# Second-layer blocks, a table load and a score bound moved inside the window-attention layer of a four-layer convolution kernel

## The chip, the cores and the metric

The kernel runs on one core of a Trainium2 chip. The metric is the device time of one execution in microseconds (us), lower being better. The engines are called by the profile's names: PE (TensorE matmuls) and PEld (its weight loads), DVE (VectorE), ACT (ScalarE), POOL (GpSimd) and SP (SyncE, which issues transfers).

## The reference, cut to what matters

Four layers run one after the other on x, of 4 images, 16 channels, 512 x 512, in fp32. Only layer 0 is touched by the change:

```python
pos = depthwise_conv3x3(x)                   # per channel
x = x + pos + pos_b
win = windows_of_8x8(affine(x))              # 64 tokens each
q, k, v = qkv(win)                           # 2 heads of 8 channels
out = softmax(q @ k.T) @ v                   # scores, exp, sums, division
x = x + proj(out)
h1 = gelu(affine(x) @ fc1_w.T + fc1_b)       # first layer, 16 -> 64
x = x + h1 @ fc2_w.T + fc2_b                 # second layer, 64 -> 16
```

Layer 1 rounds its input to 8 bits, which needs the maximum of |x| over the whole output of layer 0, then a 3x3 convolution with batch statistics. Layer 2 is two 3x3 convolutions with a residual, layer 3 a 3x3 convolution and a two-layer network with a residual.

## The kernel before

Layer 0 is `window_attention`. It takes the exponentials of the scores without subtracting a maximum first; a bound on the scores, computed on the chip from the weights and from the largest |y| seen, says at the end whether that was safe. `values_load` reads this `flag` on the engines, and a branch (L147) would run the slower `attention_block` if it weren't. Then `conv_layers` does layers 1 to 3.

The work of layer 0 is cut into 64 steps. A step n holds, for all 4 images (`u`) and 8 strips of rows (4 pairs, `vv`), one row of 8 windows. PSUM has 8 banks: banks 0 to 3 are two pairs of two, banks 4 to 7 single ones. PE, DVE, ACT and SP run the program in the order in which the Python code issues it (`manual_schedule`). A step is issued in this order:

- **Head of the step.** A table load for exp and ln (`preload_act_table_set`, L470), `values(0)` (four transposes, L346, into bank 4, copied by DVE, L351), and `scores(0)` (16 matmuls, L359, over banks 0 to 3, then two ACT exps of a pair each, L367).
- **The rest of the step before.** `output(*last)`: the second layer of image 3 of step n - 1.
- **Attention.** For k = 1 to 7: `scores(k)`, `attend(k - 1)` (L378, and the sums, L383), `values(k)`, `divide(k - 1)` (L392 to L394). In between, `turn_keys` (L318) writes the next step's keys by DMA into `y2`, and `queries` (L328) makes its queries. `project` (L402, L407) adds the result to y.
- **Second part.** 52 items go to PE in a row: 36 are depthwise taps of step n + 2 (L295, into banks 0 to 3), 16 are groups of the first layer (`hidden`, L416, each 4 matmuls into banks 4, 5, 6 in turn, and an ACT gelu, L421). Item i uses partition group i mod 4. After first-layer groups 5 and 9 stands an `output` of one image: four matmuls of 128 rows (L427) into bank 7, a DVE add to y (L429).
- **Seam.** `position(n + 2)` takes the depthwise sums out of banks 0 to 3, images 0 and 2 on DVE (L310), 1 and 3 on ACT (L306). Then comes the `output` of image 2, and the next step begins.

After the add in an odd step, `store` takes a maximum (L438) and `_store_block` issues some 16 to 19 transfers of 32 KB to `x1` from SP (L96) per image; the last step's stores are 76. Each matmul in fp32 shows as two records, so the profile counts eight L427 records per image.

Of the kernel before, what the change touches and what calls it, by code (L numbers as in the profile page):

```python
# [1 line left out]

# [9 lines left out]
F32 = mybir.dt.float32  # L12
BF16 = mybir.dt.bfloat16
AF = mybir.ActivationFunctionType
ALU = mybir.AluOpType
AX = mybir.AxisListType
# [8 lines left out]
P = 128  # L25
# [5 lines left out]
NH, HD = 2, 8  # L31
WS = 8
# [51 lines left out]
        nc.sync.dma_start(part[:, at : at + m, :], src[:, a : a + m, :])  # L84


def _store_block(nc, x1, src, b, r0, cols):

    n = WS // 2
    s, m = divmod(r0 // 2, M)  # L90
    parts = [(1, m, s, 0, n), (0, m + 1, s, 0, n)]
    if m + n == M and s < S - 1:
        parts[1:] = [(0, m + 1, s, 0, n - 1), (0, 0, s + 1, n - 1, 1)]
    for r, mm, ss, at, k in parts:
        part = 32 * b + C * r
        nc.sync.dma_start(  # L96
            x1[mm : mm + k, part : part + C, ss, cols].rearrange("m c x -> c m x"),
            src.rearrange("c (m r) x -> c m r x", r=2)[:, at : at + k, 1 - r],
        )
# [53 lines left out]
def window_attention(ctx: ExitStack, tc, xw, x1, hots, m, v, peak):  # L153
# [14 lines left out]
    nc = tc.nc  # L168
    U = V = 4
    BW = 64  # L170
    NJ = BW // WS
    N = NJ * T
    XW = 2 * BW
    SR = H // 8
    NQ = W // XW
    STEPS = SR // WS * NQ * 2

    wts = ctx.enter_context(tc.tile_pool(name="w0w", bufs=1))
# [5 lines left out]
    def bank(i):  # L184
        return pairs[i // 2][:, i % 2, :] if i < 4 else singles[i - 4]

    def quad(i):
        return slice(32 * i, 32 * i + 32)
# [43 lines left out]
    with tc.tile_pool(name="w0s", bufs=1) as scratch:  # L232
# [10 lines left out]
        size = wts.tile([P, NH + 1], F32, name="size")  # L243
# [27 lines left out]
    px = ctx.enter_context(tc.tile_pool(name="w0x", bufs=2))  # L271
# [10 lines left out]
    most = pa.tile([P, STEPS], F32, name="most")  # L282

    def by_window(ap):
        return ap.rearrange("p (j a x) -> p a j x", a=WS, x=WS)
# [29 lines left out]
    def turn_keys(y, vv):  # L315
        for u in range(U):
            for w in range(2):
                nc.sync.dma_start(  # L318
                    y2[32 * u + C * w : 32 * u + C * w + C, vv, :, w, :],
                    y[32 * vv + C * w : 32 * vv + C * w + C, u, :].rearrange(  # L320
                        "p (j t) -> p j t", t=T
                    ),
                )

    def queries(y, h):
        for u in range(U):
            for vv in range(V):
                nc.tensor.matmul(  # L328
                    bank(vv)[quad(u)], wg[h][quad(vv)], y[quad(vv), u, :],
                    start=True, stop=True,  # L330
                )
        for vv in range(V):
            out = g[:, vv, :, h, :]
            src = bank(vv).rearrange("p (j t) -> p j t", t=T)
            if vv % 2:
                nc.scalar.activation(out, src, AF.Identity, bias=gb[:, h : h + 1])
            else:
                nc.vector.tensor_scalar(out, src, gb[:, h : h + 1], None, ALU.add)


    def values(k, n):

        vv, jl = k // 2, 4 * (k % 2)
        b = bank(4 + 2 * (k % 2))
        for jj in range(4):
            nc.tensor.transpose(  # L346
                b[:, P * jj : P * jj + P],
                y2[:, vv, jl + jj].rearrange("p w t -> p (w t)"), m("ident"),
            )
        t = px.tile([P, 4, P], F32, tag="yt", name=f"yt{n}_{k}", bufs=3)  # L350
        nc.vector.tensor_copy(t.rearrange("p j c -> p (j c)"), b)  # L351
        return t
# [45 lines left out]
    def project(y):  # L398
        for h in range(NH):
            for u in range(U):  # L400
                for vv in range(V):
                    nc.tensor.matmul(  # L402
                        bank(4 + u)[quad(vv)], wo[h][quad(u)], o[quad(u), vv, :, h, :],
                        start=h == 0, stop=h == 1,
                    )
        for u in range(U):
            nc.vector.scalar_tensor_tensor(  # L407
                y[:, u], bank(4 + u), pb, y[:, u], ALU.add, ALU.add
            )

    def hidden(y, q, n):

        u, vv = q // 4, 3 * q % 4
        b = bank(4 + q % 3)
        for k in range(4):
            nc.tensor.matmul(  # L416
                b[quad(k)], fc1[quad(vv), quad(k)], y[quad(vv), u, :],
                start=True, stop=True,
            )
        hd = px.tile([P, N], F32, tag="hid", name=f"hid{n}_{u}_{vv}", bufs=8)  # L420
        nc.scalar.activation(hd, b, AF.Gelu, bias=f1b)  # L421
        return vv, hd

    def output(y, xo, hids, u, n):
        b = bank(7)
        for vv, hd in hids:
            nc.tensor.matmul(b[quad(vv)], m("fc2"), hd, start=True, stop=True)  # L427
        at = BW * (n % 2)
        nc.vector.tensor_tensor(  # L429
            xo[:, u, :, at : at + BW].rearrange("p a (j x) -> p a j x", x=WS),  # L430
            by_window(b), by_window(y[:, u]), ALU.add,
        )
        if n % 2:
            store(xo, n // 2, u)

    def store(xo, k, u):
        i, cb = divmod(k, NQ)
        nc.vector.tensor_reduce(  # L438
            peak[:, U * k + u : U * k + u + 1], xo[:, u], AX.XY, ALU.max,
            apply_absolute_value=True,  # L440
        )
        for vv in range(V):
            for w in range(2):
                r = SR * (2 * vv + w) + WS * i
                _store_block(
                    nc, x1, xo[32 * vv + C * w : 32 * vv + C * w + C, u], u, r,
                    slice(XW * cb, XW * cb + XW),
                )

    ctx.enter_context(  # L450
# [14 lines left out]
    for h in range(NH):  # L465
        queries(ys[0], h)
    last, xo = None, None
    for n in range(STEPS + 1):
        if n < STEPS:
            nc.scalar.preload_act_table_set("natural_log_exp_and_others")  # L470
            yts = {0: values(0, n)}
            es = {0: scores(0, n)}
        if last:

            output(*last)
        if n == STEPS:
            break
        for k in range(1, 8):
            es[k] = scores(k, n)
            attend(es[k - 1], yts[k - 1], k - 1)  # L480
            yts[k] = values(k, n)
            divide(k - 1, n)
            if k == 3:
                nc.vector.tensor_reduce(
                    most[:, n : n + 1], ys[n], AX.XY, ALU.max, apply_absolute_value=True
                )
            if k % 2 and n + 1 < STEPS:
                turn_keys(ys[n + 1], k // 2)
        if n + 1 < STEPS:
            queries(ys[n + 1], 0)  # L490
        attend(es[7], yts[7], 7)
        divide(7, n)
        if n + 1 < STEPS:
            queries(ys[n + 1], 1)
        y = ys.pop(n)
        project(y)

        ahead = n + 2 < STEPS
        if ahead and n % 2 == 0 and n // 2 + 2 < STEPS // 2:
            xts[n // 2 + 2] = load(n // 2 + 2)  # L500
        if n % 2 == 0:
            xo = px.tile([P, U, WS, XW], F32, tag="xo", name=f"xo{n}", bufs=1)


        hids, taken = [], [0] * U
        for i in range(13 * 4):
            q, rest = divmod(i - 4, 3)
            if i >= 4 and rest == 0 and q < 16:
                hids.append(hidden(y, q, n))
                if q in (5, 9):  # L510
                    output(y, xo, hids[q - 5 : q - 1], q // 4 - 1, n)
            elif ahead:
                depthwise(n + 2, taken[i % 4], i % 4)
                taken[i % 4] += 1
        if ahead:
            ys[n + 2] = position(n + 2)
        output(y, xo, hids[8:12], 2, n)
        last = (y, xo, hids[12:], U - 1, n)

    top = wts.tile([P, 1], F32, name="top")
    nc.vector.tensor_reduce(top, most, AX.X, ALU.max)
    ytop = wts.tile([P, 1], F32, name="ytop")
    nc.gpsimd.partition_all_reduce(ytop, top, P, bass_isa.ReduceOp.max)
    sized = wts.tile([P, NH + 1], F32, name="sized")
    nc.gpsimd.partition_all_reduce(sized, size, P, bass_isa.ReduceOp.add)
    bound = wts.tile([P, 1], F32, name="bound")
    nc.vector.tensor_tensor(bound, sized[:, 0:1], sized[:, 1:2], ALU.max)
    nc.vector.tensor_scalar(bound, bound, ytop, sized[:, 2:3], ALU.mult, ALU.add)  # L530
    nc.vector.tensor_scalar(bound, bound, ytop, 1.0 / 8.0, ALU.mult, ALU.mult)
    flag = wts.tile([P, 1], mybir.dt.int32, name="flag")
    nc.vector.tensor_scalar(flag, bound, 40.0, None, ALU.is_le)
    return nc.values_load(flag[0:1, 0:1], min_val=0, max_val=1)


# [798 lines left out]
```

## Time and profile before

| What | Value |
|---|---|
| Median of 3 runs | 6498.27 us (6492.53 to 6499.6) |
| The profiled execution's own time | 6499.56 us |
| Its span, first to last instruction | 6497.8 us |
| Mean granted PE clock | 0.981 |
| PE busy | 6264.0 us (96%) |
| ACT busy | 4179.7 us (64%) |
| DVE busy | 3186.5 us (49%) |
| POOL busy | 6.0 us |
| A step of layer 0 | 54.16 us (1612.33 to 1666.49) |
| Layer 0 | until about 3538 us, then layers 1 to 3 from 3561 us |

The span has 40 slices of 162 us; layer 0 fills the first 21 and a half. A timeline row gives the start of a group of like instructions, the time from its first start to its last end, the engine, the line, the operation, the tile written and read, the count and, in brackets, how long the engine sat idle before it and who released it. The busy share of PE counts a matmul from start to a modelled end, so a PE that is nearly always busy may still be used in part[...].

### The profile page before, as it was taken

How to read it: one execution, taken by the hardware profiler on the slowest of the kernel's cores; microseconds unless marked ns; L12 is line 12 of the kernel's file. 1: busy time of each engine (PE TensorE's matmuls, PEld its weight loads, DVE VectorE, ACT ScalarE, POOL GpSimd, SP SyncE). 2: the span in 40 equal slices, each digit the busy share in tenths (PEclk: the TensorE clock that was granted, in tenths of full speed). 3: DMA queues.
4: the chain of work that ended last, by engine and by line, in shares of the span. 5: the costliest groups of instructions: out<-in, count | busy, mean ns of one | idle time of the engine just before them, and what ended most of it. 6: DMA issues, size and time to landing. Idle time of an engine off the chain costs nothing. (4 is left out here: it accounts for less than half of the span.)

```text
span 6497.8 us, 317055 instructions
## 1 busy us (share of the span) xinstructions
PE 6264.0 (96%) x146976; PEld 3402.1 (52%) x146976; DVE 3186.5 (49%) x4640; ACT 4179.7 (64%) x5738; POOL 6.0 (0%) x26
## 2 busy tenths in 40 slices
PE   8999999999999999999997669999999999999999
PEld 5555555555555555555553335455555554555553
DVE  3444444444444444444443974544445554545554
ACT  5777777777777777777775544555555555555554
POOL 0000000000000000000000000000000000000000
PEclk9999999999999999999997879999999999999999
DMA  3333333333333333333322842222222222222221
GB/s 82 62 71 62 71 63 70 63 70 63 70 63 70 63 70 62 71 61 72 60 56 61 298 161 75 81 82 86 83 82 81 82 83 82 84 83 81 81 65 48
DMA packets 544390, 515.30 MB, mean 79 GB/s; under 512 B 349008, under 2 KB 480208, under 8 KB 514384
## 3 DMA queue, kind: packets, MB, share of 16 engines
q1 hardware_dynamic: 542768, 494.52, 29.2%
q8 instruction: 1154, 18.91, 1.2%
q14 instruction: 180, 1.47, 0.1%
q10 hardware_dynamic: 288, 0.39, 0.0%
HBM read 225.87 MB, written 134.48 MB: 55 GB/s over the span
## 5 line engine op out<-in xcount | busy, mean ns | idle before, releaser
L1123 ACT ACTIVATE hid<-tb,vec 128x512 f32<-128x512 f32 x1280 | 847.5, 687 | 1127.8 <-PE tb L1117 1126.5
L1117 PE MATMUL tb<-y,mat 32*32 32x512 f32 x16384 | 1567.9, 599 | 2.0 <-DVE o L1139 1.3
L367 ACT ACTIVATE e<-pair 128x1024 f32<-128x1024 f32 x1024 | 992.3, 1021 | 225.0 <-PE pair L359 224.3
L1125 DVE TENSOR_SCALAR hid<-tb,vec 128x512 f32<-128x512 f32 x768 | 575.3, 749 | 890.0 <-PE tb L1117 872.8
L295 PE MATMUL pair<-x,taps 32*32 32x512 f32 x18432 | 965.8, 605 | 1.9 <-ACT y L306 1.3
L416 PE MATMUL bank<-y,fc_e 32*32 32x512 f32 x8192 | 878.4, 607 | 3.7 <-ACT hid L421 3.2
L421 ACT ACTIVATE hid<-bank,f1b 128x512 f32<-128x512 f32 x1024 | 679.6, 686 | 298.8 <-PE bank L416 285.3
L351 DVE COPY yt<-bank 128x512 f32<-128x512 f32 x512 | 353.8, 691 | 906.1 <-PE bank L346 905.8
L359 PE MATMUL pair<-g,y 32*128 32x128 f32 x16384 | 651.2, 285 | 40.4 <-ACT e L367 39.3
L1117 PEld LDWEIGHTS tb<-y,mat 32*32 32x32 f32 x16384 | 496.4, 103 | 329.4 <-issue 185.0
L908 PE MATMUL tb<-z,cw 32*32 32x512 f32 x12864 | 640.4, 603 | 4.2 <-ACT z L1054 3.4
L359 PEld LDWEIGHTS pair<-g,y 32*128 32x128 f32 x16384 | 540.2, 186 | 186.8 <-ACT e L367 109.2
L908 PE MATMUL tb<-x,cw 32*32 32x512 f32 x12480 | 620.0, 597 | 1.5 <-ACT z L1054 1.5
L295 PEld LDWEIGHTS pair<-x,taps 32*32 32x32 f32 x18432 | 459.3, 103 | 286.3 <-issue 182.9
L908 PE MATMUL tb<-h,cw 32*32 32x512 f32 x12672 | 590.7, 601 | 1.8 <-ACT z L1054 1.5
L378 PE MATMUL bank<-e,yt 128*32 128x128 f32 x16384 | 555.3, 276 | 0.9 <-ACT r L393 0.9
L908 PE MATMUL tb<-q,cq 32*32 32x512 bf16 x12672 | 418.5, 424 | 138.4 <-ACT q L987 103.2
L383 PE MATMUL bank<-e,hot 128*32 128x512 f32 x4096 | 535.0, 593 | 0.0
L378 PEld LDWEIGHTS bank<-e,yt 128*32 128x32 f32 x16384 | 417.6, 109 | 108.1 <-DVE yt L351 52.8
L1133 PE MATMUL tb<-hid,mat 128*32 128x512 f32 x4096 | 471.1, 601 | 0.0
L429 DVE TENSOR_TENSOR xo<-bank,y 128x512 f32<-128x512 f32 x256 | 177.1, 692 | 547.2 <-PE bank L427 545.5
L346 PEld LDWEIGHTS bank<-mat,y 128*128 128x128 f32 x2048 | 215.3, 141 | 431.7 <-issue 378.1
(150 smaller groups left out, 6661.2 us busy)
## 6 DMA issues: line engine op xcount, KB each, us to landing
tx<-x SPq DMA_DIRECT2D x128, 1024.0 KB
x<-in_xw_dram SPq DMA_DIRECT2D x32, 2600.0 KB
y<-y SPq DMA_DIRECT2D x2048, 32.0 KB
xi<-x SPq DMA_DIRECT2D x1024, 64.0 KB
out_dram<-o SPq DMA_DIRECT2D x64, 1024.0 KB
x<-xo SPq DMA_DIRECT2D x2000, 32.0 KB
tx<-x SPq DMA_DIRECT2D x4, 768.0 KB
x<-xo SPq DMA_DIRECT2D x48, 24.0 KB
```

What stands on the lines that cost most here:

```text
L295: nc.tensor.matmul(bank(u)[quad(vv)], taps[quad(u), tap, :], xts[n // 2][quad(u), vv, dy : dy + WS, at : at + BW], start=tap == 0, stop=ta ...
L359: nc.tensor.matmul(bank(u)[:, P * jj : P * jj + P], y2[quad(u), vv, jl + jj].rearrange("p w t -> p (w t)"), g[quad(u), vv, jl + jj].rearra ...
L367: nc.scalar.activation(e[:, 2 * i : 2 * i + 2].rearrange("p u j t -> p u (j t)"), pairs[i], AF.Exp,)
L378: nc.tensor.matmul(b[quad(u), P * jj : P * jj + P], yt[:, jj, quad(u)], e[:, u, jj, :], start=True, stop=True,)
L383: nc.tensor.matmul(d[quad(u)], own, e[:, u].rearrange("p j t -> p (j t)"), start=True, stop=True,)
L416: nc.tensor.matmul(b[quad(k)], fc1[quad(vv), quad(k)], y[quad(vv), u, :], start=True, stop=True,)
L421: nc.scalar.activation(hd, b, AF.Gelu, bias=f1b)
L908: nc.tensor.matmul(p[i][_quad(j)], weights[_quad(i), side, dx, :], src[side][_quad(i), j, dx : dx + W], start=side == 0 and dx == 0, stop= ...
L1117: nc.tensor.matmul(p[_quad(c)], w1[_quad(b), 1 - par, 32 * c : 32 * c + 32], inner(ys(mm + par))[_quad(b), s, :], start=True, stop=True,)
L1123: nc.scalar.activation(hd, p, AF.Relu, bias=v("l3_b1"))
L1125: nc.vector.tensor_scalar(hd, p, v("l3_b1"), 0.0, ALU.add, ALU.max)
L1133: nc.tensor.matmul(p[_quad(b), :], w2[:, par], hd, start=par == 0, stop=par == 1)
```

## The change

It has five parts, all in layer 0.

- `output` takes several images and banks at once. In the second part the outputs of images 1 and 0 stand together after first-layer group 10, into banks 6 and 7, in place of one after group 5 and one after group 9. `hid` gets 12 buffers instead of 8.
- Image 2's output leaves the end of the step and stands with image 3's behind the next step's `scores(0)`, into banks 6 and 7.
- The table load for exp and ln is issued behind the last gelu, ahead of `position(n + 2)`, instead of at the head of the next step.
- The score bound (`bounded`) is computed behind `project` of the last step instead of after all steps.
- The stores of the last step alternate between the queues of SP and POOL.

```diff
-def _store_block(nc, x1, src, b, r0, cols):
+def _store_block(nc, x1, src, b, r0, cols, queues=None):
...
-        nc.sync.dma_start(
+        (next(queues) if queues else nc.sync).dma_start(
...
-        hd = px.tile([P, N], F32, tag="hid", name=f"hid{n}_{u}_{vv}", bufs=8)
+        hd = px.tile([P, N], F32, tag="hid", name=f"hid{n}_{u}_{vv}", bufs=12)
...
-    def output(y, xo, hids, u, n):
-        b = bank(7)
-        for vv, hd in hids:
-            nc.tensor.matmul(b[quad(vv)], m("fc2"), hd, start=True, stop=True)
+    def output(y, xo, hids, us, banks, n):
+
+        for k, (vv, hd) in enumerate(hids):
+            nc.tensor.matmul(
+                bank(banks[k // 4])[quad(vv)], m("fc2"), hd, start=True, stop=True
+            )
         at = BW * (n % 2)
-        nc.vector.tensor_tensor(
-            xo[:, u, :, at : at + BW].rearrange("p a (j x) -> p a j x", x=WS),
-            by_window(b), by_window(y[:, u]), ALU.add,
-        )
-        if n % 2:
-            store(xo, n // 2, u)
+        for u, i in zip(us, banks):
+            nc.vector.tensor_tensor(
+                xo[:, u, :, at : at + BW].rearrange("p a (j x) -> p a j x", x=WS),
+                by_window(bank(i)), by_window(y[:, u]), ALU.add,
+            )
+            if n % 2:
+                store(xo, n // 2, u)
+
+    def bounded():
...
+        nc.vector.tensor_reduce(top, most, AX.X, ALU.max)
+        ytop = wts.tile([P, 1], F32, name="ytop")
+        nc.gpsimd.partition_all_reduce(ytop, top, P, bass_isa.ReduceOp.max)
...
+        return flag
+
+
+    queues = itertools.cycle((nc.sync, nc.gpsimd))
...
-                    slice(XW * cb, XW * cb + XW),
+                    slice(XW * cb, XW * cb + XW), queues if k == STEPS // 2 - 1 else None,
...
     last, xo = None, None
+    nc.scalar.preload_act_table_set("natural_log_exp_and_others")
     for n in range(STEPS + 1):
         if n < STEPS:
-            nc.scalar.preload_act_table_set("natural_log_exp_and_others")
             yts = {0: values(0, n)}
             es = {0: scores(0, n)}
...
         project(y)
+        if n + 1 == STEPS:
+            flag = bounded()
...
-                if q in (5, 9):
-                    output(y, xo, hids[q - 5 : q - 1], q // 4 - 1, n)
+                if q == 10:
+
+
+                    output(y, xo, hids[4:8] + hids[0:4], (1, 0), (4 + 8 % 3, 7), n)
...
+        if n + 1 < STEPS:
+            nc.scalar.preload_act_table_set("natural_log_exp_and_others")
         if ahead:
             ys[n + 2] = position(n + 2)
-        output(y, xo, hids[8:12], 2, n)
-        last = (y, xo, hids[12:], U - 1, n)
...
+        last = (y, xo, hids[8:], (2, 3), (6, 7), n)
+
     return nc.values_load(flag[0:1, 0:1], min_val=0, max_val=1)
```

The removed block after the loop is the body that `bounded` now holds, with the same operations. The added import of `itertools` moves every later line by one; some lines move by more.

More of the change, by code (lines that the diff above doesn't have):

```diff
@@ L1 @@
+import itertools
 from contextlib import ExitStack
@@ L419, in hidden @@
             )
-        hd = px.tile([P, N], F32, tag="hid", name=f"hid{n}_{u}_{vv}", bufs=8)
+        hd = px.tile([P, N], F32, tag="hid", name=f"hid{n}_{u}_{vv}", bufs=12)
         nc.scalar.activation(hd, b, AF.Gelu, bias=f1b)
         return vv, hd
-    def output(y, xo, hids, u, n):
-        b = bank(7)
-        for vv, hd in hids:
-            nc.tensor.matmul(b[quad(vv)], m("fc2"), hd, start=True, stop=True)
-        at = BW * (n % 2)
-        nc.vector.tensor_tensor(
-            xo[:, u, :, at : at + BW].rearrange("p a (j x) -> p a j x", x=WS),
-            by_window(b), by_window(y[:, u]), ALU.add,
-        )
-        if n % 2:
-            store(xo, n // 2, u)
+    def output(y, xo, hids, us, banks, n):
[3 more added lines that the diff above has]
+            )
+        at = BW * (n % 2)
+        for u, i in zip(us, banks):
[6 more added lines that the diff above has]
+    def bounded():
+        top = wts.tile([P, 1], F32, name="top")
+        nc.vector.tensor_reduce(top, most, AX.X, ALU.max)
+        ytop = wts.tile([P, 1], F32, name="ytop")
+        nc.gpsimd.partition_all_reduce(ytop, top, P, bass_isa.ReduceOp.max)
+        sized = wts.tile([P, NH + 1], F32, name="sized")
+        nc.gpsimd.partition_all_reduce(sized, size, P, bass_isa.ReduceOp.add)
+        bound = wts.tile([P, 1], F32, name="bound")
+        nc.vector.tensor_tensor(bound, sized[:, 0:1], sized[:, 1:2], ALU.max)
+        nc.vector.tensor_scalar(bound, bound, ytop, sized[:, 2:3], ALU.mult, ALU.add)
+        nc.vector.tensor_scalar(bound, bound, ytop, 1.0 / 8.0, ALU.mult, ALU.mult)
+        flag = wts.tile([P, 1], mybir.dt.int32, name="flag")
+        nc.vector.tensor_scalar(flag, bound, 40.0, None, ALU.is_le)
+        return flag
+    queues = itertools.cycle((nc.sync, nc.gpsimd))
     def store(xo, k, u):
@@ L514, in window_attention @@
                 taken[i % 4] += 1
+        if n + 1 < STEPS:
+            nc.scalar.preload_act_table_set("natural_log_exp_and_others")
         if ahead:
             ys[n + 2] = position(n + 2)
-        output(y, xo, hids[8:12], 2, n)
-        last = (y, xo, hids[12:], U - 1, n)
[L522 to L533, printed above, removed]
+        last = (y, xo, hids[8:], (2, 3), (6, 7), n)
     return nc.values_load(flag[0:1, 0:1], min_val=0, max_val=1)
```

## The prediction

> **What bounds the kernel now.** I read the page first, then the windows over layer 0, then the timeline of one steady step (1599 to 1653 us), and last the timeline of the end of layer 0. The page's busy shares don't say where a step waits; its slices show TensorE nearly always busy at full clock up to one dip, which is the passage from layer 0 to layer 1.
>
> ```profile
> PE   8999999999999999999997669999999999999999
> PEclk9999999999999999999997879999999999999999
> ```
>
> Layer 0 takes 64 steps of 54.16 us (the table load at the head of the second part comes at 1612.33 and again at 1666.49). In the attention part a block of scores, attention and transposes repeats every 3.56 us, set by PE. The change leaves it alone. It touches two other places. The first is inside the second part, where an L427 block (second layer) stands between L295 (depthwise) and L416 (first layer):
>
> ```profile
> 1616.57 0.70 PE L416 MATMUL bank<-y,fc_e 32*32 32x512 f32 x4
> 1617.20 1.07 PE L427 MATMUL bank<-hid,mat 128*32 128x512 f32 x8
> 1618.19 0.67 PE L295 MATMUL pair<-x,taps 32*32 32x512 f32 x8
> ```
>
> One matmul lasts 0.59 us, so the first row's last start is 1616.57 + 0.70 - 0.59 = 1616.68. From there to the next start of small matmuls, at 1618.19, is 1.51 us. The second place is the seam of steps, here with ACT and PE together:
>
> ```profile
> 1628.13 0.69 ACT L421 ACTIVATE hid<-bank,f1b 128x512 f32<-128x512 f32 x1 [0.29 <-PE bank L416]
> 1628.14 1.06 PE L427 MATMUL bank<-hid,mat 128*32 128x512 f32 x8
> 1628.75 1.27 ACT L306 ACTIVATE y<-pair,vec 128x512 f32<-128x512 f32 x2
> 1629.13 0.66 PE L346 MATMUL bank<-mat,y 128*128 128x128 f32 x4
> 1629.72 1.50 PE L359 MATMUL pair<-g,y 32*128 32x128 f32 x32
> 1630.03 1.28 ACT L470 ACT_TABLE_LOAD   x1
> 1631.15 1.06 PE L427 MATMUL bank<-hid,mat 128*32 128x512 f32 x8
> 1631.33 1.94 ACT L367 ACTIVATE e<-pair 128x1024 f32<-128x1024 f32 x2
> 1632.40 0.49 PE L359 MATMUL pair<-g,y 32*128 32x128 f32 x4 [0.18 <-ACT e L367]
> 1633.32 1.16 PE L359 MATMUL pair<-g,y 32*128 32x128 f32 x28 [0.42 <-ACT e L367]
> ```
>
> The reader should see a chain on ACT without a hole: last gelu, two positions, table load, two exps. ACT goes into L306 the moment the gelu ends, so it isn't waiting for PE there. The table load costs nothing on PE, because PE runs scores(0) (L359) under it: scores end at 1631.22 and the table at 1631.31. Then scores(1) wait for the exps that free the pairs. So at the seam ACT sets the end, and PE has holes. Counted from T = 1627.62, the last start of a small matmul (L295), attention on chunk 0 (L378, 1634.40) begins at T + 6.78, which is 0.51 to the gelu, 0.62 gelu, 1.28 positions, 1.30 load, 1.99 exps to the scores they release, 1.08 scores(1).
>
> The end of layer 0 is held by the store queue:
>
> ```profile
> 3518.46 38.19 SPq L96 DMA_DIRECT2D x<-xo  x76
> 3537.79 0.15 DVE L533 TENSOR_SCALAR flag<-bound 128x1 int32<-128x1 f32 x1
> 3561.47 0.19 POOL L947 MEMSET q<- 128x8 bf16 x3 [24.28 <-SPq L147]
> ```
>
> The flag is ready at 3537.9; SP issues its 76 stores, 0.50 us each, until 3556.65, and layer 1 begins some 4.5 us after that.
>
> **What the skill says.** (1) TensorEngine Tiling (Array Packing), Key Properties: "Mode switching requires drain". The trace agrees: PE gaps stand around each L427 block and nowhere between L295 and L416. (2) ScalarE: Activation LUTs, Rules for kernel authors, budgets about 2.7 us for a switch of table set. The trace has 1.28 us, and I use that. (3) TensorE: Matmul & The Clock Gate, Part 1: the clock falls to half after one idle window of about 3.4 us, and the window is free-running. The trace agrees in kind: in step 62, without depthwise work, dense matmuls end at 3452, and by 3457.42 an L427 block takes 1.94 us instead of 1.06. (4) DMA: Bandwidth & Descriptors, Anatomy of one DMA: a DMA from GpSimd has about 2.0 us of fixed time, most of it completion. No run here shows such a DMA yet.
>
> **The change, part by part.**
>
> (a) *One block of two images in place of two blocks.* An ordinary item (four matmuls of one kind) takes 0.252 us: 20 items start from 1622.58 to 1627.62. A single block adds 1.51 - 0.25 = 1.26 us, of which its two passes are 0.86 us (L427 streams 512 columns in 0.43 us). A double block adds 1.26 + 0.86 = 2.12; two singles add 2.52. Saved: 0.40. Adding up the three stretches of the part item by item (20 + 15 items at the same pace, a block of 1.86, 17 items) gives 0.57. I take **0.45 us a step**, bounds 0.2 and 0.6. Bank 6 now carries image 1 and is wanted by first-layer group 11. Its add runs 1.16 to 1.85 us after the block's start (1617.20 to 1618.36 and 1619.05), and the block lasts 1.86 with two depthwise items behind it, so nothing waits. Twelve hid buffers cover eleven live tiles; cost nothing. The gelus keep pace without the early block: 0.65 us against 0.76 for three items.
>
> (b) *The third image's block leaves the end of the part and joins the fourth between scores(0) and scores(1).* Its 0.99 us goes from before the transposes (L346) into a hole. By itself this gains at most the holes, and since ACT is the chain, about nothing: the transposes still wait for the last gelu's bank.
>
> (c) *The table load in front of the positions.* In the issue order of the changed kernel ACT has gelu, table load, the two positions, exp. The same 1.28 us now delays what PE waits for. With the same T: gelu ends T + 1.15, load T + 2.43, positions T + 3.71; image 3's score waits for the second position, it may go at T + 3.80. Behind that score on PE stand all the others and the double block; behind the load on ACT stand both positions and then the exp; who waits for PE is the exp. PE has then issued transposes and one score only; about 26 of the 32 L359 records follow, 0.85 us, plus 0.3 to the exp. So exp(0) begins at T + 4.95, against T + 3.71. The load is no longer under the scores; the scores now come after it. **Loss 1.2 us a step** in 62 steps (the last two have no positions to make). Bounds: 0.85 (the records alone) to 1.3. The double block takes 1.86 of the 1.94 us of exps, so it fits there and adds nothing.
>
> (d) *Clock.* From T + 0.6 to T + 3.8 PE has only 0.66 us of transposes and one score. Of the possible phases of a 3.4 us window, those starting between about T - 0.1 and T + 1.1 hold hardly more work than this, 1.2 of 3.41, or 35% of seams. A drop lasts one window at half clock; the scores, and the double block that then takes up to 3.7 us, come about 1 us late. 62 x 0.35 x 1.0 = **22 us**. Bounds: 0 (no drop) and 62 x 0.5 x 1.3 = 40.
>
> (e) *Stores.* In odd steps the image-2 stores begin some 4.5 us later, with 16 x 0.5 = 8 us per image on SP, and the key turns (L318) queue behind them. They shift from 1709 to about 1714, the first being read at the next step's transposes near 1737; the load of x behind them is used a hundred us later. Nothing.
>
> (f) *The bound worked out earlier.* Five small DVE operations (1.0 us) and two GpSimd reductions (0.35 each) move behind the last project. DVE then sits idle for 6.0 us before L429, which covers them and their waits. What leaves the end was hidden under SP. Nothing.
>
> (g) *The last stores on two queues.* SP has 38 x 0.50 = 19 us and is done near 3540. GpSimd starts its 38 near 3520.9. The price is unknown: 0.50 as on SP gives 3540 and 16 us gained; 2.08 in series (2.0 + 32 KB at the page's rate) gives 3600 and 43 lost. The page puts most of that in completion, which can overlap, so I estimate 0.9 us: 3555, **2 us gained**.
>
> **Sum**, against the profiled execution's 6499.56: 62 x (1.2 - 0.45) = +46.5, clock +22, stores -2: 6566. The median of the runs shown is 1.3 lower, so 6565. A measurement of this kernel can tell about 0.2%, 13 us, from no change.
>
> **Rivals.** *Faster, the load hidden:* if the last gelu ended 1.28 us before the positions' matmuls, the load would fill a hole; the seam would then gain 0.1, with 0.45 from (a): 62 x 0.55 + 2 = 36 us, 6462. For it: ACT has holes of about 0.3 us before gelus. Against it: L306 starts at the gelu's end. It decides when ACT is idle for more than about 0.75 us before L306; it is idle for 0. Chance 0.10. *Slower, without clock drops:* 6565 - 22 = 6543, 0.30. For it: all of layer 0 runs at 1.00. Against it: the new hole is over three times the old one of 0.9 us. *GpSimd in series:* +45, 6610, 0.05. *The halves cancel* (saving at 0.6, loss near 0.85, no drops): about 62 x 0.25 - 16, no change, 0.05. The forecast keeps 0.50.
>
> **Numbers.** Faster 0.10, same 0.05, slower 0.85. Range: low 62 x (0.85 - 0.45) - 2 = +23, 6521; high 62 x (1.3 - 0.4) + 40 + 8 = +104, 6602, rounded to 6515 and 6605.
>
> **What would show it.** Right: L306 begins 1.3 us after the last gelu's end, L359's first records split by a wait for L306, exp(0) some 1.2 us later from the last L295, one L427 row of x16 per place, PEclk under 10 tenths in parts of layer 0, steps of about 55 us. Wrong: exp(0) no later from T, or a second part shortened by over 1 us.

## The result and the profile after

The changed kernel is slower by 0.44%: 6523.59 us median against 6495.2 for the kernel before in the same comparison, ratio 1.0044, interval 1.0034 to 1.0054. The forecast was 6565 us, with a range of 6515 to 6605. The sign came true and the time lies in the range, near its lower end, but a loss of 67 us was expected and 28 came.

The profiled executions have spans of 6497.8 and 6522.8 us, 25.0 apart. First, two rows of the page's 40 slices. The dip, where layer 0 ends, begins in the same slice as before, with an 8 in place of a 7:

```profile
PE   8999999999999999999998669999999999999999
PEclk9999999999999999999998679999999999999999
```

Next, the second part of a step in the timeline of PE. The second row is the double block:

```profile
1801.40 0.66 PE L417 MATMUL bank<-y,fc_e 32*32 32x512 f32 x4
1801.98 1.92 PE L428 MATMUL bank<-hid,mat 128*32 128x512 f32 x16
1803.84 0.66 PE L296 MATMUL pair<-x,taps 32*32 32x512 f32 x8
```

From the last small matmul's start (1801.40 + 0.66 - 0.59 = 1801.47) to the next small one it is 2.37 us, so the block adds 2.37 - 0.25 = 2.12, the number of the forecast.

Then a seam, PE and ACT in one timeline:

```profile
1753.17 1.35 ACT L422 ACTIVATE hid<-bank,f1b 128x512 f32<-128x512 f32 x2
1754.54 1.28 ACT L544 ACT_TABLE_LOAD   x1
1754.58 0.66 PE L347 MATMUL bank<-mat,y 128*128 128x128 f32 x4 [0.15 <-ACT hid L422]
1755.84 1.26 ACT L307 ACTIVATE y<-pair,vec 128x512 f32<-128x512 f32 x2
1756.58 1.74 PE L360 MATMUL pair<-g,y 32*128 32x128 f32 x32 [1.34 <-ACT y L307]
1758.17 1.94 ACT L368 ACTIVATE e<-pair 128x1024 f32<-128x1024 f32 x2 [1.07 <-PE pair L360]
1758.24 1.92 PE L428 MATMUL bank<-hid,mat 128*32 128x512 f32 x16
1760.10 1.22 PE L360 MATMUL pair<-g,y 32*128 32x128 f32 x32
1761.25 1.08 PE L379 MATMUL bank<-e,yt 128*32 128x128 f32 x32
```

The table load now stands between gelu and positions. PE's scores sit idle for 1.34 us with L307 as the releaser, and ACT, which had gone from load to exp without a hole, has one of 1.07 us while the scores run. The last gelu starts at 1753.17 + 1.35 - 0.69 = 1753.83, attention on chunk 0 at 1761.25: 7.42 us, where it was 1628.13 to 1634.40, 6.27 us.

Last, the end of layer 0:

```profile
3552.73 0.15 DVE L454 TENSOR_SCALAR flag<-bound 128x1 int32<-128x1 f32 x1
3561.44 19.76 SPq L97 DMA_DIRECT2D x<-xo  x38
3561.72 19.56 POOL L97 DMA_DIRECT2D x<-xo  x38 [9.58 <-DVE xo L433]
3585.49 0.19 POOL L962 MEMSET q<- 128x8 bf16 x3 [4.20 <-SPq L148]
```

Both queues issue 38 stores in under 20 us, 0.51 to 0.52 us each; layer 1 begins 4 us behind them.

Taken over all steps (a step is counted from one gelu table load to the next, the seam from the last gelu's start to attention on chunk 0, the second part from the first depthwise matmul to the last gelu's start; medians):

| | before | after |
|---|---|---|
| second part, to the last gelu | 17.17 us | 16.47 us |
| seam, from the last gelu | 6.25 us | 7.42 us |
| last small matmul, from the last gelu | -0.49 us | -0.01 us |
| step | 54.12 us | 54.59 us |
| steps 0 to 60, sum over that median | 0.6 us | 11.8 us |
| table load of step 62 to layer 1 | 108.65 us | 92.49 us |

The difference of the spans is then 62 x 0.47 = +29.1, slow steps +11.2, end of layer 0 -16.2, and +0.8 in the start and layers 1 to 3: 24.9 of 25.0.

### The profile page after: what moved, and what is told of

It reads as the page before. It is cut to its first block, busy times and chain, and to the rows that moved or that the text cites. A ratio compares the mean times of both kernels' runs of the same rounds, so it can differ in the third digit from the quotient of the medians.

```text
span 6522.8 us, 316735 instructions
## 1 busy us (share of the span) xinstructions
PE 6251.1 (96%) x146976; PEld 3486.9 (53%) x146976; DVE 3191.4 (49%) x4640; ACT 4185.8 (64%) x5738; POOL 25.6 (0%) x64
## 5 line engine op out<-in xcount | busy, mean ns | idle before, releaser
L417 PE MATMUL bank<-y,fc_e 32*32 32x512 f32 x8192 | 838.1, 602 | 2.4 <-ACT hid L422 1.5
L296 PEld LDWEIGHTS pair<-x,taps 32*32 32x32 f32 x18432 | 525.6, 103 | 227.6 <-issue 103.4
L923 PE MATMUL tb<-q,cq 32*32 32x512 bf16 x12672 | 435.3, 449 | 114.8 <-ACT q L1002 85.3
```

The source lines that it names most:

```text
L296: nc.tensor.matmul(bank(u)[quad(vv)], taps[quad(u), tap, :], xts[n // 2][quad(u), vv, dy : dy + WS, at : at + BW], start=tap == 0, stop=ta ...
L417: nc.tensor.matmul(b[quad(k)], fc1[quad(vv), quad(k)], y[quad(vv), u, :], start=True, stop=True,)
L923: nc.tensor.matmul(p[i][_quad(j)], weights[_quad(i), side, dx, :], src[side][_quad(i), j, dx : dx + W], start=side == 0 and dx == 0, stop= ...
```

## The experiments

The theory after this reading: the seam hangs on the last gelu and runs along ACT; the load ahead of the positions lengthens it by 1.17 us; the double block in the second part lets the last gelu come 0.70 us sooner; the slow steps are clock drops from the thin stretch of PE; the end is the store queues. Rivals: that PE sets the seam, and that the slow steps or the end have other causes.

**The table load alone**, in the kernel before:

```diff
         if n < STEPS:
-            nc.scalar.preload_act_table_set("natural_log_exp_and_others")
...
+        if n + 1 < STEPS:
+            nc.scalar.preload_act_table_set("natural_log_exp_and_others")
         if ahead:
             ys[n + 2] = position(n + 2)
```

The load for the first step stands ahead of the loop.

> The kernel before, with one edit: the table load stands ahead of the positions. Theory (the seam is a chain on ACT that starts at the last gelu; the load ahead of the positions puts scores(0) behind it instead of beside it): from the start of the last gelu to attention on chunk 0 it was 6.25 us before and 7.42 in the changed kernel, so here 7.4 too, a step of about 55.3 us, 62 x 1.17 = +73 us, near 6568, and up to 20 more where the clock drops. Rival (PE sets the seam, and the load falls into a hole): from gelu to attention up to 6.5, under +16 us.

Measured: 6565.31 us, ratio 1.0108 (1.0092 to 1.0123). The step is 55.28 us, 1.16 more than before; the second part is unchanged at 17.17, the seam 7.42. Its timeline of the seam:

```profile
1661.44 0.69 ACT L421 ACTIVATE hid<-bank,f1b 128x512 f32<-128x512 f32 x1 [0.29 <-PE bank L416]
1661.48 1.07 PE L427 MATMUL bank<-hid,mat 128*32 128x512 f32 x8
1662.15 1.28 ACT L516 ACT_TABLE_LOAD   x1
1663.44 1.26 ACT L306 ACTIVATE y<-pair,vec 128x512 f32<-128x512 f32 x2
1664.18 1.74 PE L359 MATMUL pair<-g,y 32*128 32x128 f32 x32 [1.06 <-ACT y L306]
1665.78 1.94 ACT L367 ACTIVATE e<-pair 128x1024 f32<-128x1024 f32 x2 [1.07 <-PE pair L359]
```

The whole loss per step of the changed kernel's seam is this one edit, with the same waits (L306 ahead of the scores, the scores ahead of the exps). No step dropped in clock here. Image 2's block still stands in the hole, which fits, but isn't tested by itself.

**The changed kernel with the load back at the head** of the next step:

> The changed kernel with one part undone: the table load is back at the head of the next step. Theory: the last gelu stays 0.7 us sooner after the first depthwise matmul than in the kernel before, and from it to attention on chunk 0 it is 6.25 to 6.3 us as before, because the double block (1.86 us) fits under the two exps (1.94). A step of 53.4 us, 62 x 0.7 = 43 less, and 16 from the end of layer 0: about 6435, 0.991 of before, with no clock drops. Rival (the double block or the third image's block makes PE the bound of the seam): steps of about 54.1, near 6479.

Measured: 6461.93 us, ratio 0.9941 (0.9928 to 0.9955), a step of 53.65 us. The time falls between the theory (6435) and the rival (6479). The gelu stays 0.7 sooner, and no matmul in steps 0 to 60 ran at half speed, but the seam is 6.48 and not 6.25. The two positions of ACT take 1.45 us in place of 1.27:

```profile
1673.82 1.27 PE L296 MATMUL pair<-x,taps 32*32 32x512 f32 x10
1674.37 1.52 DVE L311 TENSOR_SCALAR y<-pair,vec 128x512 f32<-128x512 f32 x2 [1.29 <-PE pair L296]
1675.15 1.45 ACT L307 ACTIVATE y<-pair,vec 128x512 f32<-128x512 f32 x2
```

The last depthwise matmul ends at 1675.09. DVE's second position starts at 1674.37 + 1.52 - 0.75 = 1675.14 and ends at 1675.89, and ACT's second starts at 1675.15 + 1.45 - 0.69 = 1675.91, 0.03 us behind. In each of steps 2 to 59 the trace has DVE's end as what released it. So a second chain, from the last depthwise matmul over DVE, ends last here, and 0.47 of the 0.70 us is kept. In the changed kernel the same chain is done before ACT's first position starts at 1755.84, since the table load stands in between:

```profile
1753.68 1.53 DVE L311 TENSOR_SCALAR y<-pair,vec 128x512 f32<-128x512 f32 x2 [3.58 <-PE pair L296]
```

A further 6 us stand in six slow steps at full clock, whose cause I didn't follow.

**The double block in the second part alone**, with image 2's output left at the end of the step:

```diff
-                if q in (5, 9):
-                    output(y, xo, hids[q - 5 : q - 1], q // 4 - 1, n)
+                if q == 10:
+                    output(y, xo, hids[4:8] + hids[0:4], (1, 0), (6, 7), n)
```

> The kernel before with the outputs of images 1 and 0 in one block behind first-layer group 10, and image 2 left where it was. Theory (it is the last gelu that counts, which comes 0.7 us sooner): the seam follows the gelu, but for the block of image 2 ahead of the transposes, which then makes PE about 0.1 late; a step of 53.5 us, 62 x 0.6 = 37 less, near 6458. Rival (what counts is the last small matmul of the second part, which came only 0.22 sooner): 14 less, near 6481.

Measured: 6472.25 us, ratio 0.9964 (0.9951 to 0.9977), second part 16.47, seam 6.48, step 53.65. By the median step the gain is 0.47 us, 29 in 62 steps: between theory (0.6) and rival (0.22), short of the theory by the same wait of the positions (here too ACT's second starts 0.03 us after DVE's second ends, in the median). The medians of the runs are 24 us apart.

**The seam's double block alone**, image 2 with image 3 behind `scores(0)`:

```diff
-        output(y, xo, hids[8:12], 2, n)
-        last = (y, xo, hids[12:], U - 1, n)
+        last = (y, xo, hids[8:], (2, 3), (6, 7), n)
```

> The kernel before with one edit: image 2's output stands with image 3's behind scores(0), in one double block. Theory (the seam hangs on the last gelu, and the double block takes 1.86 of the 1.94 us of the exps): from gelu to attention 6.25 to 6.3 us as before, steps of 54.1 to 54.2, no gain: 6493 to 6503. Rival (PE sets the seam, so that 0.99 us of work put into a hole is 0.99 us gained): 6436.

Measured: ratio 0.9999 (0.9991 to 1.0008), seam 6.24, step 54.12. Nearly a microsecond of PE work per step was put where PE stood idle, and nothing came of it. PE doesn't set this seam.

**Two queues and the early bound**, in the kernel before, and **two queues alone**, the bound left at the end:

> The kernel before with the last stores on two queues and the bound computed behind the last project, nothing else. Theory (a store takes 0.51 us to issue on either queue, and layer 1 starts 4 to 5 us after the last issue): 16 to 19 us less, near 6478; steps stay at 54.12 us. Rival (the changed kernel gained this by its shorter last step, not by the queues): under 5 us less.

> The kernel before with the last stores on two queues, the score bound left at the end. Theory (the two reductions of the bound stand on GpSimd behind its 38 stores, and the flag behind them): layer 1 starts 1.5 to 2 us later than with the bound computed early (88.7 us from the table load of step 62): about 90.5, near 6482. Rival (the order on GpSimd doesn't matter, the flag is waited for elsewhere anyway): no difference, 6480.

Measured: 6480.77 us, ratio 0.998 (0.997 to 0.999), and 6482.85, 0.9982 (0.9974 to 0.999). In the profiles the two differ by 8.6 us from the table load of step 62 on (88.70 and 97.31), but 7.95 of that is step 62 itself, which ran at full clock in one (50.54 us to the next table load) and partly at half in the other (58.49). From the first store to layer 1 it is 43.0 us in the kernel before, 30.4 with both edits, 31.0 with the queues alone. So by one profile of each kernel the queues are worth 12 us in this order of images, and the early bound 0.6, less than the theory's 1.5 to 2. Here is the bound's place on GpSimd, of the kernel with the queues alone:

```profile
3534.48 9.70 POOL L97 DMA_DIRECT2D x<-xo  x19 [2.54 <-DVE xo L430]
3544.21 0.31 POOL L528 PARTITION_ALL_REDUCE ytop<-top  x1
3551.13 0.20 POOL L950 MEMSET q<- 128x8 bf16 x3 [6.60 <-SPq L148]
```

The reduction stands behind the stores, as expected, but the rest of the way to layer 1 is mostly there in any case. In the changed kernel the stores start later and closer together, since images 1 and 0 and images 2 and 3 come in pairs; from its first store to layer 1 it is 24.0 us.

**The slow steps.** A seam of the changed kernel that is one of them:

```profile
1812.93 1.94 ACT L368 ACTIVATE e<-pair 128x1024 f32<-128x1024 f32 x2 [1.07 <-PE pair L360]
1813.00 3.20 PE L428 MATMUL bank<-hid,mat 128*32 128x512 f32 x16
1816.13 1.52 PE L360 MATMUL pair<-g,y 32*128 32x128 f32 x32
```

The double block takes 3.20 us in place of 1.92, past the end of the exps. From here matmuls last nearly twice as long for about 3 us. In steps 0 to 60 the profile has five such stretches, one of double length; the kernel before has none. They start at 117.07, 1813.50, 1868.11, 3124.22 and 3182.24, and these times lie on one grid: each distance is a whole number of spans of 3.413 us (1813.50 to 3124.22 is 384 of them). Here are windows on this grid. After their length comes PE's busy time; the third number from the end is the granted clock:

```profile
1810.09:1813.50 3.41, 2.08 (x40) 1.47 (x44) 0.69 (x1) 2.33 (x4) 0.00 (x0) 1.00 0.35 65
1813.50:1816.91 3.41, 3.41 (x28) 1.11 (x24) 2.33 (x3) 1.36 (x2) 0.00 (x0) 0.50 0.38 70
3011.58:3015.00 3.42, 2.18 (x42) 0.85 (x11) 2.19 (x3) 3.39 (x5) 0.00 (x0) 1.00 0.29 54
3066.19:3069.61 3.42, 2.15 (x40) 0.83 (x11) 2.19 (x3) 3.39 (x5) 0.00 (x0) 1.00 0.62 141
3120.81:3124.22 3.41, 2.12 (x40) 0.81 (x10) 2.19 (x3) 3.38 (x5) 0.00 (x0) 1.00 0.37 71
3124.22:3131.05 6.83, 6.62 (x56) 3.34 (x60) 2.00 (x3) 2.67 (x4) 0.00 (x0) 0.50 0.35 65
```

In this profile the clock is at half after each of the five windows in which PE is busy for 2.12 us or less, and after no window with 2.15 or more (only the stretch of double length goes on past a fuller one). First I moved the double block of images 2 and 3 ahead of the transposes, into the hole:

> The changed kernel with one edit: the double block of images 2 and 3 stands ahead of the transposes, so it fills the hole of PE in which it waits for the positions. Theory: the chain on ACT is as before the edit, since the scores wait for the positions anyway: 7.4 us from the last gelu to attention, a step of 54.6 us; but the slow steps (the changed kernel's profile has six of them, 11.8 us over the median step in all) are clock drops of that hole and go, so that the sum over the median step falls under 3 us and the time is 6510 to 6515. Rival (the slow steps come from elsewhere): as many of them, near 6523. Second rival (PE sets the seam): each step longer by 0.5 us or more.

Measured: 6522.81 us, ratio 1.0044 (1.0028 to 1.0059), step 54.59, seam 7.41, and six stretches at half speed. The chain was right, the clock wrong: the block leaves its old place between scores(0) and scores(1), where a hole opens in turn (PE waits 0.93 us for the exps there). The test moved the hole and so doesn't decide. Then I kept everything and filled the hole with useless work:

```diff
             yts = {0: values(0, n)}
+            for r in range(2 if 0 < n else 0):
+                for jj in range(4):
+                    nc.tensor.transpose(
+                        bank(7)[:, P * jj : P * jj + P],
+                        y2[:, 0, jj].rearrange("p w t -> p (w t)"), m("ident"),
+                    )
             es = {0: scores(0, n)}
```

> The changed kernel with useless work in the hole: the four transposes of values(0) are issued twice more, into bank 7, ahead of scores(0); their result is overwritten unread. Theory: they take 2 x 0.59 us between 1.35 and 2.74 us after the last gelu's start, where PE waits for the positions, so the chain keeps its 7.4 us and the step its 54.6; but the thin stretch of PE is now under the length that lets the clock drop: no matmul at half speed, sum of the steps over the median under 2 us in place of 11.8, 6510 to 6514. Rival (what the clock counts isn't PE work in this stretch): as many drops, near 6523.

Measured: 6514.42 us, ratio 1.0032 (1.0019 to 1.0045). The added matmuls are the second row. PE's wait for L307 shrinks from 1.34 to 0.47 us:

```profile
1753.94 0.66 PE L347 MATMUL bank<-mat,y 128*128 128x128 f32 x4 [0.17 <-ACT hid L422]
1754.43 1.04 PE L498 MATMUL bank<-mat,y 128*128 128x128 f32 x8
1755.94 1.74 PE L360 MATMUL pair<-g,y 32*128 32x128 f32 x32 [0.47 <-ACT y L307]
```

Seam and step are the same to the hundredth (7.42, 54.59), no matmul in these steps runs at half speed, the sum over the median falls from 11.8 to 3.3 us. The sum was to fall under 2 us; more than half of what is left stands in step 0, at full clock, and stays open. The thinnest window on the grid now has 2.37 us of PE in steps 0 to 60, where it was 1.81 in the changed kernel and 2.81 in the kernel before. So 8.5 of the 11.8 us go when the thin windows go, with seam and step as they were: the thin stretch of PE causes the drops in clock. This rests on one profile of each kernel. The run times alone don't show it, since the intervals of the two ratios overlap (1.0019 to 1.0045, and 1.0034 to 1.0054), though the runs draw together: six within 6512.6 to 6516.4, where those of the changed kernel lie between 6508.9 and 6532.8.

**A better version.** If the seam hangs on the last gelu, then the double block of the second part belongs behind it. From the kernel with the load back at the head:

```diff
-                if q == 10:
-                    output(y, xo, hids[4:8] + hids[0:4], (1, 0), (4 + 8 % 3, 7), n)
...
+        output(y, xo, hids[0:8], (0, 1), (7, 6), n)
         last = (y, xo, hids[8:], (2, 3), (6, 7), n)
```

with 16 hid buffers, for which the zero rows at the start are written in two halves; and then, in a second kernel, `scores(0)` ahead of `values(0)`.

> The changed kernel with the table load back at the head of the step, and the double block of images 0 and 1 moved from first-layer group 10 to the end of the second part, behind the last depthwise matmul (16 hid buffers; the zero rows at the start are written in two halves to make room). Theory (the last gelu is what the seam hangs on, and one change of tiling less): the last gelu comes 2.1 us sooner; the double block then stands between it and the transposes, so PE sets the seam: about 7.4 us from gelu to attention; a step of about 52.5 us, 1.1 under the kernel with the load at the head (53.65): near 6390. Rival (the second part is then bound by ACT's gelus, or the seam by the adds on DVE): steps of 53.4 or more, over 6445.

> As the kernel with the block last, and scores(0) stand ahead of the four transposes of values(0). Theory: the exps then start 0.6 us sooner, beside the transposes and the second double block; PE has no hole left in the seam: a step of about 52.2 us, near 6370. Rival (PE was already without a hole, so order changes nothing): within 5 us of the kernel with the block last.

Measured: 6359.71 us, ratio 0.9786 (0.9772 to 0.9799), step 51.83; and 6347.84 us, 0.9773 (0.976 to 0.9787), step 51.78. The last gelu now starts 14.0 us after the first depthwise matmul, and the seam takes 7.13 and 7.07. The first gain is larger than expected by 30 us: the gelu comes 2.5 us sooner, not 2.1, and the seam is 0.3 shorter. The second, 12 us by the medians, is under the 20 of its theory and over the 5 of its rival; only 3 of it is in the median step, the rest in fewer slow steps, and why is open. The seam of the second, PE and ACT in one timeline:

```profile
1618.58 1.28 ACT L495 ACT_TABLE_LOAD   x1
1618.71 1.17 PE L361 MATMUL pair<-g,y 32*128 32x128 f32 x32
1619.81 0.66 PE L348 MATMUL bank<-mat,y 128*128 128x128 f32 x4
1619.91 1.94 ACT L369 ACTIVATE e<-pair 128x1024 f32<-128x1024 f32 x2
1620.59 1.92 PE L429 MATMUL bank<-hid,mat 128*32 128x512 f32 x16
1622.44 1.17 PE L361 MATMUL pair<-g,y 32*128 32x128 f32 x32
1623.54 1.08 PE L380 MATMUL bank<-e,yt 128*32 128x128 f32 x32
```

No PE row has a wait in brackets, and the load stands beside the scores again.

## Why the prediction was right or wrong

- **(c), the load: right.** 1.2 us a step forecast; the seam, counted from the last gelu, is 1.17 longer in the changed kernel, and the step 1.16 longer with that edit alone. The reading that carried it (L306 begins as the gelu ends, and the load was hidden under the scores) was the right one, and the rival with the load in a hole was rightly small.
- **(b), the third image's block: right.** About nothing, and by itself a ratio of 0.9999.
- **(a), the double block, and the sum of (a) and (c): the step that failed.** The block's own cost was exact, 2.12 us. But "with the same T" failed: all times of the seam were counted from the last small matmul, with the gelu 0.51 us behind it. The last small matmul came only 0.22 us sooner, the last gelu 0.70, since the last first-layer group, on which it waits, came 0.73 us sooner. So the forecast's own sign, exp(0) some 1.2 us later from the last L295, did not come: it was 3.71 us and is 4.34. With the load ahead of the positions the seam hangs on the gelu, and it is 0.70 that counts in place of 0.45. The net step is 1.17 - 0.70 = 0.47, not 0.75: 17 us of the error. The two parts were also added as if each stood alone. Each alone was priced well, 1.16 for the load and 0.47 for the double block, which would make 0.69 a step; together they cost 0.47, because the table load covers DVE's wait for the last depthwise matmul. That makes 14 of the 17 us. That 0.47 alone is so near the forecast's 0.45 is partly luck, since the 0.45 was meant for T, which moved by 0.22.
- **(d), the clock: right in kind, twice too large.** 22 us in 22 seams forecast, 1.0 us each; slow steps made 11.2 us more than before, most of it in five steps with half clock, at about 2 us each. The count was some four times too high and the price per drop half of what it was, and the two errors partly cancel. The forecast took all phases of the window as equally likely. But a step of 54.59 us is nearly 16 windows of 3.413 (54.61), so successive seams meet nearly the same phase, and the window creeps by some 0.025 us a step: the rows 54.61 us apart show 2.18, 2.15 and 2.12 us of PE, and only the last brings a drop. So a drop comes only where this creep has carried a window far enough onto the hole. What starts and ends such a series, no run here shows. The Trainium skill (TensorE: Matmul & The Clock Gate, Part 1) has a free-running window of 3.4 us, which fits the grid here.
- **(g), the two queues: price wrong.** 0.9 us per store from GpSimd was an estimate; the trace has 0.51, nearly as from SP. From the first store to layer 1 it is 24.0 us in place of 43.0, and the first store comes 2.8 us later after the table load of step 62, so the end gained 16.2 us and not 2: 14 us of the error. The Trainium skill (DMA: Bandwidth & Descriptors, Anatomy of one DMA) puts most of a transfer's fixed 2 us in completion, and 38 stores issued 0.51 us apart agree with that; the lower price, 0.50, was the better reading of it.
- **(e) and (f): right.** The kernel with the seam's double block alone moves image 2's stores too, and its step stays at 54.12 us. The early bound is worth 0.6 us, in one profile of each kernel.

Together 17 + 11 + 14 = 42 us, less the 0.8 elsewhere: the forecast's +66.5 against the 25.0 of the spans. All three errors had one direction. That the time still lies in the range is luck: its lower end stood for a load that costs only 0.85 us, no drop in clock and 2 us at the end, and none of these came.

## What to carry to other kernels

Count a stage from the event on which its chain hangs, in the changed kernel the last gelu, not from the last instruction of the busiest engine: an edit can move the two apart by half a microsecond. When two edits touch one seam, ask which chain ends last with both in place, before their prices are added. A load or table switch that runs beside another engine's work costs nothing until it is moved ahead of what that engine waits for. And when ACT holds a seam, move whatever PE can do late behind ACT's last input: the same double block was worth 0.47 us a step in the middle of the part and 1.8 us more at its end.

## What the runs showed of the hardware

In the changed kernel's profile the clock fell to 0.50 for a window of 3.41 us after windows in which PE was still busy for 1.81 to 2.12 us, so a window need not be empty for this, and it kept 1.00 after one with 2.15. No single bound of busy time holds for all kernels here: the one with the block moved ahead of the transposes dropped after windows of 2.05 to 2.30 us and kept its clock after one of 2.20, and the one with the table load alone kept it after one of 2.07. Eight useless matmuls (1.04 us in the row above) kept the clock up in the profile that has them, with seam and step unchanged. GpSimd issued 32 KB stores at 0.51 us each, SP at 0.52.
